# Two-layer cross-attention and feed-forward kernel: a scale folded into its weights, forty early zero-matmuls, constants by reductions, another order

## The chip, the cores and the metric

The kernel runs on one core of one Trainium2 chip. The metric is device time in microseconds (us), the median of several runs. A core has five engines that work side by side, each through its own queue and in order: TensorE (PE, matrix products), VectorE (DVE), ScalarE (ACT), GpSimd (POOL) and SyncE (SP, which here issues the transfers). They wait for each other by semaphores.

## The reference

The input x has 128 sequences of 64 tokens with 128 features; the context has the same shape. Four blocks follow each other, each added to x:

```
x = x + xattn0(layernorm(x), ctx, ctx)   # 16 heads of 8; q, k, v from normalised inputs;
                                         # softmax(q k^T / sqrt(8)) v; @ Wo + bo;
                                         # times sigmoid(qn @ Wg), then a layer norm
x = x + ffn0(layernorm(x))               # h = silu(w1 x * s1) * (w2 x * s2)
                                         # h = gelu(h1 h * s); h = gelu(h2 h * s)
                                         # out = (w3 h) * w3_s
x = x + xattn1(layernorm(x), ctx, ctx)   # 16 heads, plain softmax attention, @ w_o^T + b_o
x = x + ffn1(layernorm(x))               # relu(x W1 + b1) W2 + b2
```

The ffn weights h1 and h2 are 512 x 512, w3 is 128 x 512. `w3_s` is a vector of 128 factors, one for each output feature, so it may be applied to the output or to the columns of the weights.

## The kernel before, in words

The 8192 tokens are cut into 17 chunks: one of 256 tokens, fifteen of 512, one of 256. Each chunk goes through four stages, written as Python generators: `attention0`, `ffn0`, `attention1`, `ffn1`. A chunk of 512 tokens has two halves in each attention. All weights stay in on-chip memory; x, context and work tiles rotate through numbered slots.

A half of an attention goes like this. Scores come from PE (L658). DVE takes the negated maximum over keys (L662). DVE or POOL splits it into three bf16 parts (L672 to L675). PE transposes these (L679), ACT copies the result (L682). PE computes the scores again, transposed, with the maximum subtracted (L691). ACT exponentiates (L696). PE multiplies with the values (L710). ACT and DVE sort out the two heads that share a tile (L720 to L724), DVE takes the reciprocal of the sums (L727, L728), POOL multiplies (L742), and PE applies the output weights (L770). A layer norm is moments on DVE (L541, L543), an inverse root on POOL (L526 to L559) and the scaling on ACT (L568) or DVE (L572). PE transposes the result (L582).

In `ffn0` the two first products are L903 and L904, tanh is on ACT (L907), the gating on DVE (L909, L910). The square products are done with seven block products instead of eight (L956), for which POOL forms differences of inputs (L938) and sums of weights (L896). At its end the product with w3 (L770) stands in a PSUM bank. DVE multiplies it by `w3_s` into a work tile (L1046), and POOL adds that tile to x (L1048). In `ffn1` the products are L1080 and L770.

The order of all instructions is planned when the program is built. The class `Order` keeps a clock for each engine and for each slot, and gives each operation a length from a table (`LENGTHS`). Of all operations whose inputs are planned, it issues next the one that can start first; ties go by priority. To that priority a random draw is added, seeded by one number for each stretch of 50 us of planned time (`DRAWS`; a seed of 0 adds nothing). What comes out is one fixed queue for each engine.

At the start PE has nothing to do, so it multiplies a tile of zeros (L428): 60 matmuls before anything else, and more wherever the plan shows PE idle in its first 95 us (`RAMP`). Constants are made on DVE meanwhile: `masks` sums a table of 0 and 1 over two of its axes (L479 to L483), `folds` adds column groups of the identity (L799 to L804) and widens the result to `asel` (L808). POOL blanks three value tiles with memsets (L496, L498).

Of the kernel before, what the change touches and what calls it, by code (L numbers as in the profile page):

```python
# [26 lines left out]
HS = 4  # L27
# [11 lines left out]
for _n, _w in _COLS:  # L39
# [10 lines left out]
N_VB, N_NM = 3, 4  # L50
# [11 lines left out]


STRETCH = 50.0
DRAWS = [97, 0, 427, 0, 249, 0, 0, 0, 575, 0, 0, 112, 0, 817, 0, 39, 412, 0, 615, 329, 0, 15, 762, 0]
SPREAD = 0.1
SWAP = [*range(16, 32), *range(16)]

# [2 lines left out]
PE, DVE, ACT, POOL, SP = "PE", "DVE", "ACT", "POOL", "SP"  # L71
NONE = ""
# [8 lines left out]
        "product": (0.865, -0.2), "f1": (0.865, -0.2),  # L81
    },
    DVE: {
        "bias+": 0.28, "masks": 1.2, "gate weights": 0.4, "folds": 1.9, "moments": 1.07, "z": 1.3, "copied": 0.68,
        "scaled": 0.75, "qx": 1.5, "kx": 1.5, "vb": 1.8, "max": 2.3, "parts": 0.8, "reciprocal": 2.2, "o2": 0.83,
        "from bank": 0.68, "gate sums": 1.3, "gate": 0.4, "gained": 1.1, "gated": 1.45, "sum": 0.68, "saved": 0.68,
        "relu": 0.7,
# [235 lines left out]
def kernel(  # L323
# [16 lines left out]
    nc = tc.nc  # L340
# [7 lines left out]
    const = ctx.enter_context(tc.tile_pool(name="const", bufs=1))  # L348
# [8 lines left out]
    def tile_of(slot, shape, dtype=F32):  # L357

        kind, i = slot
        n = 1  # L360
        for d in shape[1:]:
            n *= d
        if kind == "bank":
            t = banks[:, i, :]
            t = t[:, 0:n] if dtype is F32 else t.bitcast(dtype)[:, 0:n]
        else:
            t = work.tile([P, COLUMNS[kind]], dtype, tag=f"{kind}{i}", name=f"{kind}{i}")[:, 0:n]
        if len(shape) == 2:
# [37 lines left out]
    order = Order(RESOURCES)  # L406
# [3 lines left out]
    hm = load("hm", [P, 2, 2, 2], headmask.rearrange("p (n s t) -> p n s t", n=2, s=2))  # L410
# [7 lines left out]
    w3 = load("w3", [P, 4, D], w_3)  # L418
# [7 lines left out]
    def busy(n, bank):  # L426
        for _ in range(n):
            nc.tensor.matmul(banks[:, bank, 0:P], blank, blank, start=True, stop=True)  # L428

    order.busy = busy  # L430
    busy(60, 7)
    ident = const.tile([P, P], F32, tag="ident", name="ident")
    make_identity(nc, ident)

    mask = const.tile([P, 4], F32, tag="mask", name="mask")
    half_mask = const.tile([P, 2, 4], F32, tag="half_mask", name="half_mask")
    im, pm = (lambda i: mask[:, i : i + 1]), (lambda i: mask[:, 2 + i : 3 + i])
    neg_half = const.tile([P, NG], F32, tag="neg_half", name="neg_half")
    nc.gpsimd.memset(neg_half, -0.5)
# [19 lines left out]
    def rowv(name, ng):  # L459
        return each(row[:, ROW[name], :], ng)  # L460
# [15 lines left out]

    def masks():
        yield Op(DVE, "masks")
        nc.vector.tensor_tensor(half_mask[:, 0, 0:2], hm[:, 0, 0, :], hm[:, 0, 1, :], ALU.add)  # L479
        nc.vector.tensor_tensor(half_mask[:, 1, 0:2], hm[:, 1, 0, :], hm[:, 1, 1, :], ALU.add)  # L480
        nc.vector.tensor_tensor(half_mask[:, 0, 2:4], hm[:, 0, :, 0], hm[:, 0, :, 1], ALU.add)
        nc.vector.tensor_tensor(half_mask[:, 1, 2:4], hm[:, 1, :, 0], hm[:, 1, :, 1], ALU.add)
        nc.vector.tensor_tensor(mask, half_mask[:, 0, :], half_mask[:, 1, :], ALU.add)  # L483
        for t, i, name in (
            (bk0, 2, "L0_xattn_bk"), (bq0, 0, "L0_xattn_bq"), (bk1, 2, "L1_xattn_b_k"), (bq1, 0, "L1_xattn_b_q"),
        ):
            nc.vector.tensor_scalar(t, mask[:, i : i + 2], colv(name), None, ALU.mult)

    def blanks():

        for i in range(N_NM):
            yield Op(POOL, "blank", put=[("nm", i)])
            nc.gpsimd.memset(nmax[i], 0.0)
            if i < N_VB:
                yield Op(POOL, "blank values", put=[("vb", i)])
                nc.gpsimd.memset(vblk[i], 0.0)  # L496
                for par in range(2):
                    nc.gpsimd.memset(vblk[i][64 * par : 64 * par + 64, :, 1, par, :], 1.0)  # L498
# [1 line left out]
    ones = const.tile([P, P], F32, tag="ones", name="ones")  # L500
    gw = const.tile([P, D + 1], F32, tag="gw", name="gw")
    identb = const.tile([P, P], BF16, tag="identb", name="identb")
    fold = const.tile([P, 2, 32], F32, tag="fold", name="fold")
    asel = const.tile([P, HS, P], BF16, tag="asel", name="asel")
    half_s1 = const.tile([P, 4], F32, tag="half_s1", name="half_s1")
    half_s12 = const.tile([P, 4], F32, tag="half_s12", name="half_s12")
# [249 lines left out]
    def token_major(blocks, ng, free, own=False):  # L756

        pe = None
        for g in range(ng):
            op = yield Op(  # L760
                PE,
                "tokens" if len(blocks) == 1 else "tokens 4",
                get=None if pe else {"bank": 1, "wk": 1} if own else {"bank": 1},
                put=free if g == ng - 1 else (),
            )
            if pe is None:
                pe = op
                ps = tile_of(pe.slots["bank"][0], (P, ng, D))
            for n, (lhs, w) in enumerate(blocks):
                nc.tensor.matmul(  # L770
                    ps[:, g, :],
                    lhs(g),
                    w,
                    start=(n == 0),
                    stop=(n == len(blocks) - 1),
                )
        return (ps, pe.slots["bank"], pe.slots["wk"]) if own else (ps, pe.slots["bank"])
# [16 lines left out]
    def folds():  # L794

        yield Op(DVE, "folds")

        nc.vector.tensor_copy(identb, ident)
        nc.vector.tensor_tensor(  # L799
            fold, ident[:, 0:64].rearrange("p (r c) -> p r c", r=2), ident[:, 64:128].rearrange("p (r c) -> p r c", r=2), ALU.add  # L800
        )
        nc.vector.tensor_tensor(fold[:, 0, :], fold[:, 0, :], fold[:, 1, :], ALU.add)
        for j in range(1, 3):
            nc.vector.tensor_tensor(  # L804
                fold[:, 0, 0:8], fold[:, 0, 0:8], fold[:, 0, 8 * j : 8 * j + 8], ALU.add
            )
        for s in range(HS):
            nc.vector.tensor_copy(  # L808
                asel[:, s, :].rearrange("p (j k) -> p j k", j=2),
                fold[:, 0, 2 * s : 2 * s + 2].unsqueeze(2).to_broadcast([P, 2, 64]),  # L810
            )

        nc.vector.tensor_scalar(half_s1, col[:, COL["L0_ffn_w1_s"]], 0.5, None, ALU.mult)
        nc.vector.tensor_tensor(half_s12, half_s1, col[:, COL["L0_ffn_w2_s"]], ALU.mult)
# [68 lines left out]
    def weights(l):  # L883

        a = [[wh[:, l, 2 * j : 2 * j + 2, 256 * i : 256 * i + 256] for j in range(2)] for i in range(2)]
        s = [ws[:, l, n] for n in range(3)]
        for out, x, y, f in (
            (s[0], a[1][0], a[1][1], ALU.add),  # L890
            (s[1], s[0], a[0][0], ALU.subtract),
            (a[1][0], a[0][0], a[1][0], ALU.subtract),
            (s[2], a[0][1], s[1], ALU.subtract),
        ):
            yield Op(POOL, "weights")
            nc.gpsimd.tensor_tensor(out, x, y, f)  # L896

        made_weights[l] = [a[0][0], a[0][1], s[2], a[1][1], s[0], s[1], a[1][0]]

# [115 lines left out]
    def ffn0(ci, prio):  # L1015
        xt, ng = x_sb[ci], GROUPS[ci]
        z, fz = yield from normalised(xt, ng)
        zT, fz = yield from transposed(z, ng, fz)
        fz = Last(fz, 4)
        b, made = {}, []  # L1020
        n = ng * P
        yield from two_halves(b, n)
        for k in range(4):
            made.append((yield (gated(k, zT, n, fz, b), prio)))
        yield made[:1]
        h = [Both(made[0], made[1]), Both(made[2], made[3])]
# [8 lines left out]
        ps, fp, fw = yield from token_major(  # L1035
            [
                (lambda g, k=k: b[k // 2][0][:, 2 * g // ng, k % 2, g * P % (n // 2) : g * P % (n // 2) + P], w3[:, k, :])
                for k in range(4)
            ],
            ng,  # L1040
            b[0][1] + b[1][1],
            own=True,
        )
        yield Op(DVE, "from bank", put=fp)
        y = tile_of(fw[0], (P, ng, D))
        nc.vector.tensor_tensor(y, ps, rowv("L0_ffn_w3_s", ng), ALU.mult)  # L1046
        yield Op(POOL, "add", put=fw)
        nc.gpsimd.tensor_tensor(xt, xt, y, ALU.add)  # L1048


    def context1(ci, got, prio):
# [68 lines left out]
    landed = [Op(SP, "load") for _ in range(9)]  # L1120
# [76 lines left out]
```

## Time and profile before

| what | value |
|---|---|
| median of three runs | 1130.64 us (1130.12 to 1131.97) |
| the profiled execution | 1132.17 us |
| its span, first to last instruction | 1130.3 us |
| PE busy | 1100.1 us (97%), 13871 matmuls |
| weight loads on PE | 868.5 us |
| DVE busy | 866.8 us |
| ACT busy | 726.0 us |
| POOL busy | 504.9 us |
| mean granted clock of PE | 0.996 |
| transfers | 23.23 MB, mean 21 GB/s |

All durations below are of the profiled execution. "Busy" of PE counts from a matmul's start to its modelled end. The time of the whole is the span and 1.9 us around it. The "chain" of the profile is found by going back from the last instruction, at each step to what released it or to the instruction before it on its engine.

### The profile page before, as it was taken

How to read it: one execution, taken by the hardware profiler on the slowest of the kernel's cores; microseconds unless marked ns; L12 is line 12 of the kernel's file. 1: busy time of each engine (PE TensorE's matmuls, PEld its weight loads, DVE VectorE, ACT ScalarE, POOL GpSimd, SP SyncE). 2: the span in 40 equal slices, each digit the busy share in tenths (PEclk: the TensorE clock that was granted, in tenths of full speed). 3: DMA queues.
4: the chain of work that ended last, by engine and by line, in shares of the span. 5: the costliest groups of instructions: out<-in, count | busy, mean ns of one | idle time of the engine just before them, and what ended most of it. 6: DMA issues, size and time to landing. Idle time of an engine off the chain costs nothing.

```text
span 1130.3 us, 32935 instructions
## 1 busy us (share of the span) xinstructions
PE 1100.1 (97%) x13871; PEld 868.5 (77%) x13871; DVE 866.8 (77%) x2139; ACT 726.0 (64%) x1279; POOL 504.9 (45%) x882
## 2 busy tenths in 40 slices
PE   7699999999999999999999999999999999999998
PEld 6577687778876778878676887777778887789786
DVE  7887969889877777567978687788789888643773
ACT  5467767666775776576646686667867675545553
POOL 6745545445534445333326355335345546352221
PEclk9999999999999999999999999999999999999999
DMA  7001000000001001001100000000000000000001
GB/s 244 12 2 29 21 11 21 11 1 20 12 2 34 2 2 39 1 3 38 49 20 20 11 21 11 12 19 12 11 11 12 11 7 11 1 1 1 12 20 43
DMA packets 35444, 23.23 MB, mean 21 GB/s; under 512 B 1504, under 2 KB 34272, under 8 KB 35168
## 3 DMA queue, kind: packets, MB, share of 16 engines
q1 hardware_dynamic: 35296, 21.13, 6.3%
q8 instruction: 109, 1.79, 0.7%
q14 instruction: 39, 0.32, 0.1%
HBM read 16.93 MB, written 4.19 MB: 19 GB/s over the span
## 4 chain that ended last, share of the span: by engine, by line
PE 87%; DVE 9%; ACT 2%; issue 1%; POOL 1%; DVEq 0%; ACTq 0%; POOLq 0%
PE banks L956 33%; PE banks L770 12%; PE banks L691 7%; PE banks L710 5%; PE banks L658 5%; PE banks L1080 5%; PE banks L903 4%; PE banks L904 4%; PE banks L582 4%; DVE m L662 3%; PE banks L631 3%; PE banks L618 2%; PE banks L606 2%; DVE su L727 1%; PE banks L428 1%
## 5 line engine op out<-in xcount | busy, mean ns | idle before, releaser
L662 DVE TENSOR_REDUCE m<-banks 128x32 f32<-128x2048 f32 x64 | 145.9, 2281 | 17.6 <-PE banks L658 16.9
L742 POOL TENSOR_TENSOR wk<-av,rec 128x256 f32<-128x256 f32 x64 | 46.9, 733 | 220.6 <-DVE rec L728 198.0
L696 ACT ACTIVATE e<-banks 128x2048 f32<-128x2048 f32 x64 | 120.2, 1877 | 36.3 <-PE banks L691 29.1
L956 PE MATMUL banks<-hd,wh 128*128 128x256 f32 (+1 forms) x544 | 127.7, 371 | 0.4 <-DVE wk L909 0.4
L956 PE MATMUL banks<-wk,wh 128*128 128x256 f32 (+1 forms) x544 | 127.5, 371 | 0.0
L956 PE MATMUL banks<-wk,ws 128*128 128x256 f32 (+1 forms) x544 | 126.3, 371 | 0.8 <-POOL wk L938 0.7
L727 DVE RECIPROCAL su<-su 128x256 f32<-128x256 f32 x64 | 111.5, 1742 | 0.0
L956 PEld LDWEIGHTS banks<-wk,wh 128*128 128x128 f32 x544 | 96.4, 190 | 18.0 <-issue 5.7
L975 ACT ACTIVATE hd<-hd,col 128x256 f32<-128x256 f32 (+1 forms) x204 | 88.8, 488 | 31.7 <-DVE hd L982 30.9
L956 PEld LDWEIGHTS banks<-hd,wh 128*128 128x128 f32 x544 | 95.4, 190 | 16.4 <-issue 4.1
L956 PEld LDWEIGHTS banks<-wk,ws 128*128 128x128 f32 x544 | 94.7, 190 | 16.5 <-issue 3.3
L982 DVE TENSOR_TENSOR hd<-banks,hd 128x512 f32<-128x512 f32 (+1 forms) x102 | 66.7, 656 | 52.9 <-PE banks L956 45.3
L529 POOL TENSOR_TENSOR nr<-nv,neg_half 128x4 f32<-128x4 f32 (+1 forms) x102 | 99.7, 978 | 8.5
L938 POOL TENSOR_TENSOR wk<-hd,wk 128x512 f32<-128x512 f32 (+1 forms) x68 | 82.4, 1212 | 40.4 <-DVE hd L910 29.0
L512 ACT COPY hd<-banks 128x512 f32<-128x512 f32 (+1 forms) x68 | 37.9, 557 | 73.0 <-PE banks L956 67.9
L568 ACT ACTIVATE wk<-x,nb,nr 128x128 f32<-128x128 f32 x192 | 79.0, 484 | 7.1 <-POOL nb L559 6.8
L658 PEld LDWEIGHTS banks<-kx,qx 32*128 32x128 f32 x2048 | 62.8, 186 | 22.4 <-issue 10.0
L710 PEld LDWEIGHTS banks<-e,vblk 128*32 128x32 f32 x4096 | 60.2, 110 | 24.0 <-issue 7.6
L658 PE MATMUL banks<-kx,qx 32*128 32x128 f32 x2048 | 74.6, 282 | 2.5 <-ACT qx L597 1.2
L710 PE MATMUL banks<-e,vblk 128*32 128x64 f32 x4096 | 70.4, 220 | 2.2 <-ACT e L696 2.2
L691 PE MATMUL banks<-qx,kx 32*128 32x128 f32 x2048 | 71.7, 277 | 0.0
L909 DVE SCALAR_TENSOR_TENSOR wk<-wk,banks 128x512 f32<-128x512 f32 (+1 forms) x68 | 43.9, 646 | 33.1 <-ACT wk L907 33.0
(136 smaller groups left out, 2399.2 us busy)
## 6 DMA issues: line engine op xcount, KB each, us to landing
c<-in_c_dram SPq DMA_DIRECT2D x30, 256.0 KB, 3.0
x<-in_x_dram SPq DMA_DIRECT2D x15, 256.0 KB, 3.6
out_dram<-x SPq DMA_DIRECT2D x15, 256.0 KB, 2.3
wh<-in_w_h_dram SPq DMA_DIRECT2D x1, 2048.0 KB, 12.4
c<-in_c_dram SPq DMA_DIRECT2D x4, 128.0 KB, 2.7
wa<-in_w_a_dram SPq DMA_DIRECT2D x2, 256.0 KB, 5.1
w<-in_w_dram SPq DMA_DIRECT2D x1, 512.0 KB, 7.9
wf<-in_w_f_dram SPq DMA_DIRECT2D x2, 256.0 KB, 6.7
```

The lines of the kernel that those rows point to most:

```text
L529: nc.gpsimd.tensor_tensor(rs, ve, neg_half[:, 0:ng], ALU.pow)
L568: nc.scalar.activation(z[:, g, :], src[:, g, :], AF.Identity, bias=nb[:, g : g + 1], scale=rs[:, g : g + 1])
L658: nc.tensor.matmul(sc[:, g, s, :], qs[h, s, :], ks[h, s, :], start=True, stop=True)
L662: nc.vector.tensor_reduce(m, sc.rearrange("p g s (j k) -> p g (s j) k", j=2), AX.X, ALU.max, negate=True,)
L691: nc.tensor.matmul(sT[:, g, s, :], lhs, rhs, start=(n == 0 and s == 0), stop=(n == 1), skip_group_check=True)
L696: nc.scalar.activation(e.rearrange("p g s i q -> p (g s i q)"), sT.rearrange("p g s c -> p (g s c)"), AF.Exp, scale=SCALE,)
L710: nc.tensor.matmul(po[32 * g : 32 * g + 32, i, s, :], vb[:, 4 * (half * HS + s) + g, i : i + 2].rearrange("p h j d -> p (h j d)"), e[:, g, ...
L727: nc.vector.reciprocal(su, su)
L770: nc.tensor.matmul(ps[:, g, :], lhs(g), w, start=(n == 0), stop=(n == len(blocks) - 1),)
L938: nc.gpsimd.tensor_tensor(T[m][0], x(), y(), ALU.subtract)
L956: nc.tensor.matmul(pieces[bank][0][:, o], w[:, k, o * P : (o + 1) * P], x[:, k], start=(new and k == 0 and o == 0), stop=(k == 1), skip_gr ...
L975: nc.scalar.activation(out(i, t)[:, o], (src or out(i, t))[:, o], AF.Gelu, scale=colv(scale, 2 * i + o))
```

## The change

Five things change.

- `w3_s` is multiplied once into the w3 weights, on POOL, after the weight sums of the second square layer. At the end of `ffn0` one DVE addition of the PSUM bank and x takes the place of the DVE product and the POOL addition.
- PE starts with 40 zero-matmuls instead of 60, and the planner's clock of PE starts at 2.5 us instead of 0.
- `masks` and `folds` use reductions over two axes and one widening copy instead of chains of small additions; their planned lengths are lowered.
- The memset of the last value tile may be planned only from 24 us on (`landed[7]`).
- All 24 seeds of the draws are new, and none is zero, so that the planned order differs on every engine from the start to the end.

```diff
-DRAWS = [97, 0, 427, 0, 249, 0, 0, 0, 575, 0, 0, 112, 0, 817, 0, 39, 412, 0, 615, 329, 0, 15, 762, 0]
+DRAWS = [36508, 23866, 23866, 23866, 23866, 23866, 23866, 23866, 23866, 23866, 23866, 23866, 23866, 23866, 23866, 61831, 23866, 23866, 61347, 23866, 22251, 23866, 8812, 23866]
...
-    busy(60, 7)
+    busy(40, 7)
+    order.clock[PE] = 2.5
...
-        nc.vector.tensor_tensor(half_mask[:, 0, 0:2], hm[:, 0, 0, :], hm[:, 0, 1, :], ALU.add)
...
-        nc.vector.tensor_tensor(mask, half_mask[:, 0, :], half_mask[:, 1, :], ALU.add)
+        for i, order_of in ((0, "p n s t -> p t n s"), (2, "p n s t -> p s n t")):
+            nc.vector.tensor_reduce(mask[:, i : i + 2], hm.rearrange(order_of), AX.XY, ALU.add)
...
             if i < N_VB:
+                if i == N_VB - 1:
+                    yield Op(NONE, "free", after=landed[7])
                 yield Op(POOL, "blank values", put=[("vb", i)])
...
-        nc.vector.tensor_tensor(fold[:, 0, :], fold[:, 0, :], fold[:, 1, :], ALU.add)
...
+        rows_of_8 = ident.rearrange("p (r j c) -> p c r j", j=4, c=8)[:, :, :, 0:3]
+        nc.vector.tensor_reduce(fold, rows_of_8, AX.XY, ALU.add)
+        nc.vector.tensor_copy(
+            asel.rearrange("p s (j k) -> p (s j) k", j=2), fold.unsqueeze(2).to_broadcast([P, 2 * HS, SEQ])
         )
...
+        if l == 1:
+            yield Op(POOL, "weights")
+            nc.gpsimd.tensor_tensor(w3, w3, rowv("L0_ffn_w3_s", 4), ALU.mult)
...
-            own=True,
         )
         yield Op(DVE, "from bank", put=fp)
-        y = tile_of(fw[0], (P, ng, D))
-        nc.vector.tensor_tensor(y, ps, rowv("L0_ffn_w3_s", ng), ALU.mult)
-        yield Op(POOL, "add", put=fw)
-        nc.gpsimd.tensor_tensor(xt, xt, y, ALU.add)
+        nc.vector.tensor_tensor(xt, ps, xt, ALU.add)
```

More of the change, by code (lines that the diff above doesn't have):

```diff
@@ L83 @@
     DVE: {
-        "bias+": 0.28, "masks": 1.2, "gate weights": 0.4, "folds": 1.9, "moments": 1.07, "z": 1.3, "copied": 0.68,
+        "bias+": 0.28, "masks": 0.9, "gate weights": 0.4, "folds": 1.3, "moments": 1.07, "z": 1.3, "copied": 0.68,
         "scaled": 0.75, "qx": 1.5, "kx": 1.5, "vb": 1.8, "max": 2.3, "parts": 0.8, "reciprocal": 2.2, "o2": 0.83,
@@ L435 @@
     mask = const.tile([P, 4], F32, tag="mask", name="mask")
-    half_mask = const.tile([P, 2, 4], F32, tag="half_mask", name="half_mask")
     im, pm = (lambda i: mask[:, i : i + 1]), (lambda i: mask[:, 2 + i : 3 + i])
@@ L478, in masks @@
         yield Op(DVE, "masks")
-        nc.vector.tensor_tensor(half_mask[:, 0, 0:2], hm[:, 0, 0, :], hm[:, 0, 1, :], ALU.add)
-        nc.vector.tensor_tensor(half_mask[:, 1, 0:2], hm[:, 1, 0, :], hm[:, 1, 1, :], ALU.add)
-        nc.vector.tensor_tensor(half_mask[:, 0, 2:4], hm[:, 0, :, 0], hm[:, 0, :, 1], ALU.add)
-        nc.vector.tensor_tensor(half_mask[:, 1, 2:4], hm[:, 1, :, 0], hm[:, 1, :, 1], ALU.add)
-        nc.vector.tensor_tensor(mask, half_mask[:, 0, :], half_mask[:, 1, :], ALU.add)
+        for i, order_of in ((0, "p n s t -> p t n s"), (2, "p n s t -> p s n t")):
+            nc.vector.tensor_reduce(mask[:, i : i + 2], hm.rearrange(order_of), AX.XY, ALU.add)
         for t, i, name in (
@@ L502 @@
     identb = const.tile([P, P], BF16, tag="identb", name="identb")
-    fold = const.tile([P, 2, 32], F32, tag="fold", name="fold")
+    fold = const.tile([P, 2 * HS], F32, tag="fold", name="fold")
     asel = const.tile([P, HS, P], BF16, tag="asel", name="asel")
@@ L798, in folds @@
         nc.vector.tensor_copy(identb, ident)
-        nc.vector.tensor_tensor(
-            fold, ident[:, 0:64].rearrange("p (r c) -> p r c", r=2), ident[:, 64:128].rearrange("p (r c) -> p r c", r=2), ALU.add
-        )
-        nc.vector.tensor_tensor(fold[:, 0, :], fold[:, 0, :], fold[:, 1, :], ALU.add)
[L803 to L811, printed above, removed]
+        rows_of_8 = ident.rearrange("p (r j c) -> p c r j", j=4, c=8)[:, :, :, 0:3]
+        nc.vector.tensor_reduce(fold, rows_of_8, AX.XY, ALU.add)
+        nc.vector.tensor_copy(
+            asel.rearrange("p s (j k) -> p (s j) k", j=2), fold.unsqueeze(2).to_broadcast([P, 2 * HS, SEQ])
+        )
         nc.vector.tensor_scalar(half_s1, col[:, COL["L0_ffn_w1_s"]], 0.5, None, ALU.mult)
@@ L1034, in ffn0 @@
         yield ready[0] + ready[1]
-        ps, fp, fw = yield from token_major(
+        ps, fp = yield from token_major(
             [
```

## The prediction

> **What bounds the kernel now.** I read the busy shares first, then the stages, then who waited for whom on TensorE (PE), then the chain of waits through the first 100 us.
>
> ```profile
> PE 1100.1 (97%) x13871; PEld 868.5 (77%) x13871; DVE 866.8 (77%) x2139; ACT 726.0 (64%) x1279; POOL 504.9 (45%) x882
> ```
>
> PE is idle for 1130.3 - 1100.1 = 30.2 us. Nothing that the other engines save counts unless it shortens those 30 us, or takes useless instructions off PE. The stages say where they lie (after each length: busy us of PE, PEld, DVE, ACT, POOL, then the granted clock):
>
> ```profile
> 0.00:10.00 10.00, 8.74 (x104) 8.55 (x104) 6.20 (x43) 2.67 (x5) 6.68 (x22) 1.00 0.65 178
> 20.00:30.00 10.00, 7.19 (x233) 6.13 (x232) 7.71 (x21) 5.77 (x12) 3.45 (x7) 1.00 0.47 125
> 40.00:60.00 20.00, 14.95 (x152) 11.25 (x152) 16.73 (x43) 8.33 (x16) 14.82 (x30) 0.85 0.05 14
> 500.00:600.00 100.00, 96.49 (x1404) 72.83 (x1403) 81.30 (x207) 61.05 (x100) 30.66 (x54) 1.00 0.11 31
> 900.00:1000.00 100.00, 100.00 (x1191) 79.61 (x1191) 74.88 (x172) 62.05 (x102) 46.59 (x78) 1.00 0.02 6
> 1000.00:1050.00 50.00, 50.00 (x368) 44.48 (x367) 20.43 (x44) 24.95 (x59) 19.13 (x29) 1.00 0.01 1
> 1120.00:1130.30 10.30, 6.65 (x53) 5.93 (x51) 1.12 (x2) 1.64 (x4) 0.00 (x0) 0.95 0.13 40
> ```
>
> Length minus PE busy, added over all stages: 15.8 us before 100 us, 10.8 us from 100 to 1000 us, none from 1000 to 1120 us, 3.6 us at the end (last add and store, which stay). So there are two places to gain: the ramp, and some ten stalls in the middle. In the ramp PE also executes most of its 217 zero-matmuls, 17.8 us busy. The middle's stalls are these (waits of PE after 100 us: total, times, longest):
>
> ```profile
> PE banks L679 <- DVE nmax L675: 4.0, 4, 1.4
> PE banks L770 <- DVE m L662: 2.7, 1, 2.7
> PE banks L679 <- POOL nmax L675: 1.3, 2, 1.0
> ```
>
> They are the softmax maximum: scores (L658), maximum on DVE (L662), its split into parts (L672 to L675), then its transpose (L679), behind which PE's whole queue stands. The chain of the start (start, length, what):
>
> ```profile
> 0.98 6.40 PE banks L428 x67
> 7.38 0.28 PE banks L790 x2
> 7.66 1.56 PE banks L428 x28
> 9.22 0.24 PE banks L582 x2
> ...
> 50.62 1.35 ACT qx L597 x2
> 51.97 0.04 issue
> 52.01 1.22 PE banks L658 x32
> 53.25 2.30 DVE m L662
> ```
>
> Until 9 us PE is late only because of its own zeros. The first normalised tile stood ready at 6.45 us (ACT L568, 5.57 plus 0.88), and its transpose came at 9.06. Later the ramp is a chain of latencies over DVE, POOL and ACT, with PE waiting.
>
> **The change, part by part.**
>
> *Scale folded into w3.* Removed per chunk: DVE L1046 (684 ns) and POOL L1048 (1275 ns). Added per chunk: one DVE add of the nearest row's kind (L1075, 685 ns). DVE: 0. POOL: 15 x 1.275 + 2 x 0.726 = 20.6 us less, plus one 1.27 us product (row L896). POOL is 45% busy, so no time directly.
>
> ```profile
> L1048 POOL TENSOR_TENSOR x<-x,wk 128x512 f32<-128x512 f32 x15 | 19.1, 1275 | 41.9 <-DVE wk L1046 38.9 <-DVE gate L842 3.1
> L1046 DVE TENSOR_TENSOR wk<-banks,row 128x512 f32<-128x512 f32 x15 | 10.3, 684 | 18.1 <-PE banks L770 18.0
> ```
>
> Each chunk's next moments start 1.3 us earlier. DVE had waited 10.0 us for that add, 7 times, but no PE wait names it: I take 0, between 0 and 2 us of gain (a share of the 10.8). The one w3 product stands in POOL's queue after the weight sums of the second square layer and right before the parts of chunk 2's first maximum. By the stepping below it is done at 55.5 us, the parts at 56.5, while PE has other work to 57.4: 0, at most 1.3 us if that cover is gone. w3 is first read after 80 us.
>
> *Constants.* Four fold instructions (0.22, 0.20, 0.37 for two) and four copies (0.63) become one reduction over 12 of 128 columns per output and one copy; five mask sums (five of 0.15 to 0.17) become two reductions. No such small reduction is in the trace. Bounds: 0.15 us (the smallest DVE rows) and 0.3 us (96 inputs at 2281/2048 = 1.1 ns each is 0.11, plus 0.15 fixed). I take 0.25 each, and 0.5 for the copy: about 0.9 us less on DVE before 7.7 us. It is then caught by a transfer: the moments of x of chunk 1 waited for their DMA until 9.35 us. So 0, with 0.5 us either way.
>
> *Zeros: 60 became 40.* By the 107 ns pitch (49 up to 6.18 us; 56 ns after), 40 end at 5.25, the gate product (0.3) at 5.55, the next 18 at 6.9. PE is free 2.1 us earlier at this point. In all, 204 stand where 217 did.
>
> *Order.* Both programs' listings give the same useful matmuls, 350 instead of 353 changes between PE's array modes, and much moved work. Counted by rows: 18 more normalisations on DVE (0.43 each), fewer key and query maskings there: DVE about +3 us. ACT: 10 fewer table loads (1.283 each), 18 fewer normalisations, 10 more maskings: about -20 us. SP issues the same 80 instructions. The last memset of a value tile (1.38 + 0.6 us, L496 and L498) moves behind the first maximum's parts on POOL.
>
> *Ramp, stepped along the new order with these rows' durations.* x of chunk 0 now goes first through POOL: moments end at 4.80, POOL's five small steps take 1.63 (3.90 to 5.53 before), ACT 0.88: transpose at 7.6 instead of 9.06. But DVE does the query mask after x of chunk 1 (10.5), then 0.98 and 0.54; values and keys 1.15; keys' mask on ACT 1.1: first scores at 14.2, before 14.13. The lead is gone there. It returns in chunk 1: its scores come at 20.9 and 24.5 (before 22.53 and 26.18), the third maximum ends at 27.9 (before 32.1). Chunk 2's normalised context again comes late (43.6, before 43.3), since two halves' products stand ahead of its moments on DVE; PE sits about 3.5 us idle. Then the difference: chunk 0's feed-forward tile is normalised on ACT at 47.6, ahead of chunk 2's query mask instead of behind it (51.84), and the first w1 product (L903) starts at 49.9 instead of 56.56. Before, 2.4 us of chunk 2's scores had been done by then, so the true lead is 4.3 us. Chunk 2's softmax follows between the feed-forward's pieces. When chunk 1's feed-forward tile is transposed (67.6; before 70.54) PE has also done 3.4 us more useful work; before got that far at 75.9: a lead of 8.3 us. From 76.7 us to 120 us PE had no stall before, so a lead at that point is kept to the end, if the new order has no new stalls.
>
> *The clock takes a part back.* I stepped at full rate. The trace has two stretches at half rate (columns as above):
>
> ```profile
> 44.00:45.00 1.00, 0.65 (x4) 0.48 (x3) 1.00 (x2) 0.47 (x1) 1.00 (x2) 0.50 0.30 85
> 58.00:59.00 1.00, 1.00 (x5) 0.82 (x4) 0.90 (x4) 0.27 (x1) 0.78 (x4) 0.50 0.00 0
> ```
>
> They follow gaps of 1.4 us (at 40.7), and of 1.2 and 1.6 us (at 50.8 and 54.1), and each loses 1.7 us (the missing clock shares added). The Trainium skill (TensorE: Matmul & The Clock Gate, "What's actually happening") says that PE falls to half rate after an idle window of about 3.4 us. By the rule only the new order's 3.5 us gap would count: lead 8.3 - 1.7 = 6.6. By the trace shorter gaps suffice, and the new ramp has as many: 8.3 - 3.4 = 4.9. The measurement decides: 5 us, between 2 and 8. The same section asks about 3.4 us of steady work for full rate, which speaks against cutting zeros; here it took 5.2 us (0.98 to 6.18), and zeros and gate product run unbroken to 6.9. If it came a window later, 0.5 us.
>
> *Middle.* For each softmax half I added PE's work that stands between the scores and the transpose of the maximum in both listings. The chain needs about 3.5 us (2.2 + 1.1 + semaphores) if DVE is free. After the ramp, covers under 4 us: 9 halves before, 14 now; the shortest 1.9 before (the one near the 2.7 us stall), 3.4 now. So the 2.7 us stall goes, and five more short covers come, at 5.3/9 = 0.6 us each: -2.7 + 3.0 = 0. Range -8 to +10 us.
>
> *Sum.* The profiled execution took 1132.17 us, span 1130.3 plus 1.9 around it. 1132.2 - 5 + 0 = 1127.2. The median of the three runs stands 1.5 us under the profiled one: 1125.7.
>
> **Rivals.**
> 1. *The lead is lost in the ramp.* More zeros stand behind the first transpose than before (146, before 122: 24 x 0.056 = 1.3 us), and longer half-rate stretches eat the rest. For it: at the first scores my steps show no lead. Against: the feed-forward starts 4 us earlier by a plain exchange on ACT. Time about 1130.
> 2. *Slower: the maximum's transpose becomes the bound of the middle.* 14 short covers, each at the largest wait seen (1.4 us, L679), are 19.6 us instead of 10.8: +8.8, minus 5, is +3.8: 1134.5. It decides from about 1 us per short cover on. For it: DVE's order is in-line, and its 18 more normalisations stand ahead of maxima. Against: ACT and POOL are both freer by 20 us.
> 3. *The middle runs clean as well*: only 3 of 10.8 us of stalls stay: 1132.2 - 5 - 7.8 - 1.5 = 1118.
>
> **How the numbers follow.** Likeliest 0.50 (1123 to 1128); rival 3, 0.21; rival 1, 0.16; rival 2, 0.13. About 0.2% (2.3 us) can be told from no change here. Faster: 0.50 + 0.21 = 0.71; same 0.16; slower 0.13. The range runs from rival 3 with one us more of lead (1116) to a little short of rival 2 (1134).
>
> **What would show it.** Right: the first L582 near 7.6 us and first L903 near 50; all but one of the zero-matmuls before 65 us; PE idle before 100 us about 11 to 13 us; idle from 100 to 1000 us near 11 us; POOL about 486 us busy, ACT near 706. Wrong: a first L903 after 55 us, or L679 waiting more than 12 us in the middle.

## The result, and the profile after

The changed kernel takes 1136.88 us (median; 1136.32 to 1137.02) where the kernel before, run beside it, takes 1131.31 us (1130.12 to 1133.12). The ratio is 1.0043, interval 1.0031 to 1.0054: slower by 0.3 to 0.5%, where 1125.7 us had been predicted. The profiled execution took 1136.92 us with a span of 1134.9 us, 4.6 us more than before's span.

The busy shares of the changed kernel, the first line of its page:

```profile
PE 1104.3 (97%) x13858; PEld 870.4 (77%) x13858; DVE 866.4 (76%) x2139; ACT 704.5 (62%) x1252; POOL 487.2 (43%) x874
```

PE is idle for 1134.9 - 1104.3 = 30.6 us, before for 30.2 us. So nearly all of the 4.6 us is *busy* time of PE (4.2 us), with 13 matmuls fewer. PE did no more work; it did some of it more slowly. The stages show where (after each length: busy us of PE, PEld, DVE, ACT, POOL, then the granted clock):

```profile
0.00:10.00 10.00, 8.22 (x79) 7.43 (x79) 6.36 (x40) 3.49 (x6) 7.13 (x24) 1.00 0.68 191
20.00:30.00 10.00, 7.56 (x250) 6.70 (x250) 8.52 (x17) 4.67 (x8) 3.74 (x9) 1.00 0.42 115
40.00:60.00 20.00, 14.23 (x92) 9.63 (x89) 16.81 (x44) 8.37 (x17) 14.42 (x24) 0.83 0.05 14
60.00:80.00 20.00, 18.70 (x331) 16.29 (x332) 16.29 (x43) 10.21 (x18) 7.12 (x17) 0.83 0.01 2
80.00:100.00 20.00, 18.07 (x107) 13.53 (x106) 18.27 (x54) 14.78 (x36) 14.94 (x23) 1.00 0.10 27
500.00:600.00 100.00, 99.85 (x1227) 78.70 (x1226) 71.60 (x201) 68.86 (x123) 33.87 (x70) 1.00 0.12 33
900.00:1000.00 100.00, 99.47 (x1244) 77.67 (x1237) 76.70 (x168) 66.42 (x118) 43.70 (x82) 1.00 0.02 6
1000.00:1050.00 50.00, 50.00 (x362) 45.14 (x362) 21.95 (x48) 25.54 (x62) 20.72 (x29) 1.00 0.00 1
```

A granted clock of 0.83 over 20 us is a loss of 0.17 x 20 = 3.4 us, and it stands in two stages: two stretches at half rate (granted clock 0.50) of 6.8 us each (43.2 to 50.0, 60.3 to 67.1). Before had two of half that length, which lost 1.7 us each. The length less PE's busy time gives the idle time: 17.3 us before 100 us (before 15.8; 11 to 13 had been predicted), 9.3 us from 100 to 1000 us (before 10.8), none from 1000 to 1120 us, 4.0 us at the end. The middle is what was predicted, and its stalls are short and spread (waits of PE after 100 us, the three largest):

```profile
PE banks L678 <- DVE nmax L674: 1.6, 1, 1.6
PE banks L690 <- ACT e L695: 1.6, 2, 1.0
PE banks L690 <- DVE av L723: 1.1, 1, 1.1
```

To see where the lead went I added up PE's useful work (each matmul at a fixed length by its shape, zeros left out) and looked up when each amount had been reached, in us from the span's start:

| useful work done | 36 us | 45 us | 60 us | 100 us | 1031 us (nearly all) |
|---|---|---|---|---|---|
| before | 76.2 | 85.5 | 100.5 | 143.8 | 1126.3 |
| changed | 77.4 | 86.4 | 103.7 | 147.6 | 1130.5 |

At 100 us of work the changed kernel is 3.8 us behind, and from there on both need the same time (982.5 and 982.9 us). The whole loss lies in the first 148 us. Half rate is a part of it; the waits of PE between 40 and 100 us point to the rest:

```profile
PE banks L581 <- ACT wk L567: 2.6, 1, 2.6
PE banks L630 <- ACT wk L588: 1.9, 1, 1.9
PE banks L897 <- DVE wk L903: 1.6, 1, 1.6
PE banks L657 <- DVE m L661: 1.5, 1, 1.5
```

The first was foreseen (3.5 us had been predicted). The other three were not. Two of them follow one DVE group. DVE's timeline (start, length, engine, line, what), with the row of the kernel before as the last line:

```profile
52.82 4.63 DVE L563 SCALAR_TENSOR_TENSOR wk<-wk,mv,row 128x128 f32<-128x128 f32 x4
57.38 0.41 DVE L903 SCALAR_TENSOR_TENSOR wk<-wk,banks 128x256 f32<-128x256 f32 x1
57.89 0.48 DVE L904 SCALAR_TENSOR_TENSOR hd<-wk,half_s,banks 128x256 f32<-128x256 f32 x1
58.28 2.28 DVE L661 TENSOR_REDUCE m<-banks 128x32 f32<-128x2048 f32 x1
...
58.73 1.13 DVE L564 SCALAR_TENSOR_TENSOR wk<-wk,mv,row 128x128 f32<-128x128 f32 x4
```

The same four instructions take 4.63 us in place of 1.13. They scale a chunk's attention output and are wanted only at 65.9 us, but the gating (L903, L904) and the maximum (L661) stand behind them in DVE's queue. PE waits first for the gating and then for the maximum. POOL's timeline in these microseconds is one unbroken row of instructions that read and write the on-chip memory (SBUF), the new w3 product (L890) last:

```profile
52.22 1.27 POOL L839 TENSOR_TENSOR x<-x,row 128x512 f32<-128x512 f32 x1
53.44 1.32 POOL L887 TENSOR_TENSOR wh<-wh 128x512 f32<-128x512 f32 x1
54.72 1.31 POOL L887 TENSOR_TENSOR ws<-wh,ws 128x512 f32<-128x512 f32 x1
56.00 1.31 POOL L890 TENSOR_TENSOR w<-w,row 128x512 f32<-128x512 f32 x1
```

DVE's group ends at 57.45, just as POOL's row ends at 57.31. The chain that ended last runs through it (start, length, what):

```profile
52.91 4.54 DVE wk L563 x4
57.45 0.34 DVE wk L903
...
58.37 2.21 DVE m L661
60.58 0.04 issue
60.62 2.14 PE banks L657 x32
```

The third wait, 1.9 us at 96.5, has the same form. Four gate sums on DVE (L827, 0.28 us each at 71.6 us) meet three 128x512 differences of POOL:

```profile
92.54 0.42 DVE L976 TENSOR_TENSOR hd<-banks,hd 128x256 f32<-128x256 f32 x1 [0.40 <-PE banks L950]
92.88 1.00 DVE L827 SCALAR_TENSOR_TENSOR wk<-wk,gw 128x128 f32<-128x128 f32 x1
...
93.81 1.35 DVE L827 SCALAR_TENSOR_TENSOR wk<-wk,gw 128x128 f32<-128x128 f32 x1
...
95.30 1.34 DVE L827 SCALAR_TENSOR_TENSOR wk<-wk,gw 128x128 f32<-128x128 f32 x1
...
96.58 0.41 DVE L976 TENSOR_TENSOR hd<-banks,hd 128x256 f32<-128x256 f32 x1
```

```profile
92.46 1.28 POOL L932 TENSOR_TENSOR wk<-hd,hd 128x512 f32<-128x512 f32 x1
93.69 1.32 POOL L932 TENSOR_TENSOR wk<-hd 128x512 f32<-128x512 f32 x1
95.09 1.41 POOL L932 TENSOR_TENSOR wk<-hd,wk 128x512 f32<-128x512 f32 x1
```

The slow DVE instructions end within 0.15 us of POOL's ends (93.88, 95.16 and 96.64 against 93.74, 95.01 and 96.50). The fourth, not shown, started together with the last of POOL's three and took its usual 0.28 us. Behind them waits a short sum (L976), behind that on ACT a gelu (L969), behind that in ACT's queue the copy (L588) that PE's values need:

```profile
97.03 0.69 ACT L969 ACTIVATE hd<-hd,col 128x128 f32<-128x128 f32 x2 [1.68 <-DVE hd L976]
97.63 0.76 ACT L588 ACTIVATE wk<-banks,col 128x512 f32<-128x512 f32 x1
```

Before had no wait of PE above 0.4 us between 73 and 110 us.

The Trainium skill states what the rows suggest (SBUF — State Buffer, "Who interferes with whom"): a DVE instruction with two SBUF inputs contends with a GpSimd instruction that reads SBUF, and whichever comes second stands still until the other is through. L563 has its tile and the gain row in SBUF, L827 its tile and the gate weights. L976 has one input in PSUM, and its 0.42 us at 92.54 beside POOL's L932 is its usual length.

### The profile page after: what moved, and what is told of

The parts are those of the page before. It is cut to its first block, busy times and chain, and to the rows that moved or that the text cites. A ratio compares the mean times of both kernels' runs of the same rounds, so it can differ in the third digit from the quotient of the medians.

```text
span 1134.9 us, 32840 instructions
## 1 busy us (share of the span) xinstructions
PE 1104.3 (97%) x13858; PEld 870.4 (77%) x13858; DVE 866.4 (76%) x2139; ACT 704.5 (62%) x1252; POOL 487.2 (43%) x874
## 4 chain that ended last, share of the span: by engine, by line
PE 86%; DVE 9%; ACT 3%; issue 1%; POOL 0%; DMA 0%; SPq 0%; DVEq 0%; ACTq 0%
PE banks L950 33%; PE banks L769 12%; PE banks L690 6%; PE banks L657 6%; PE banks L709 5%; PE banks L1070 5%; PE banks L897 4%; PE banks L898 4%; PE banks L581 3%; PE banks L617 3%; PE banks L630 2%; PE banks L605 2%; DVE m L661 2%; DVE su L726 1%; ACT e L695 1%
## 5 line engine op out<-in xcount | busy, mean ns | idle before, releaser
L661 DVE TENSOR_REDUCE m<-banks 128x32 f32<-128x2048 f32 x64 | 146.0, 2281 | 20.6 <-PE banks L657 20.2
L969 ACT ACTIVATE hd<-hd,col 128x256 f32<-128x256 f32 (+1 forms) x204 | 88.4, 488 | 45.5 <-DVE hd L976 45.0
L976 DVE TENSOR_TENSOR hd<-banks,hd 128x512 f32<-128x512 f32 (+1 forms) x102 | 66.3, 655 | 48.0 <-PE banks L950 39.1
L932 POOL TENSOR_TENSOR wk<-hd,wk 128x512 f32<-128x512 f32 (+1 forms) x68 | 82.5, 1214 | 12.4 <-PE banks L605 3.8
L567 ACT ACTIVATE wk<-x,nb,nr 128x128 f32<-128x128 f32 x176 | 72.6, 487 | 4.6 <-POOL nb L558 4.2
L897 PE MATMUL banks<-wk,w 128*128 128x512 f32 (+1 forms) x136 | 68.6, 586 | 2.7 <-DVE wk L903 1.6
```

Of the source, the lines that this page charges most:

```text
L661: nc.vector.tensor_reduce(m, sc.rearrange("p g s (j k) -> p g (s j) k", j=2), AX.X, ALU.max, negate=True,)
L897: nc.tensor.matmul(pa, w12[:, 0, k * P : (k + 1) * P], zT, start=True, stop=True)
L932: nc.gpsimd.tensor_tensor(T[m][0], x(), y(), ALU.subtract)
L969: nc.scalar.activation(out(i, t)[:, o], (src or out(i, t))[:, o], AF.Gelu, scale=colv(scale, 2 * i + o))
```

## The experiments

All times are medians, with the ratio to the kernel before run beside each and its interval. The text before each measurement is what was expected of it. The changed kernel's own interval is 1.0031 to 1.0054. Those of experiments 1 to 3 overlap it, so their gains of 1.0 to 2.4 us are not clear of noise, and their traces say more than their times. Those of experiments 5 to 7 and 9 to 11 lie below it.

**1. POOL's sums of the second layer moved to the start.** The four sums are issued behind the last value tile's memset, and no longer at 46 to 56 us.

```diff
+                if i == N_VB - 1:
...
+                    nc.gpsimd.tensor_tensor(s[0], a[1][0], a[1][1], ALU.add)
+                    nc.gpsimd.tensor_tensor(s[1], s[0], a[0][0], ALU.subtract)
+                    nc.gpsimd.tensor_tensor(a[1][0], a[0][0], a[1][0], ALU.subtract)
+                    nc.gpsimd.tensor_tensor(s[2], a[0][1], s[1], ALU.subtract)
...
-            nc.gpsimd.tensor_tensor(out, x, y, f)
+            if l == 0:
+                nc.gpsimd.tensor_tensor(out, x, y, f)
```

> The changed kernel with its planned order, but the four weight sums of the second square layer are issued on POOL right after the last value tile's memset (about 21.7 us, where POOL waited 6 us for DVE) instead of between 46 and 56 us. Theory A (four DVE normalisations of chunk 1, L563, took 4.63 us instead of 1.13 because POOL ran without a break at 51 to 57.3 us on the same tiles' memory): they take 2 to 3 us, the third w1 product no longer waits 1.6 us, and the total falls by 1.5 to 5 us against the changed kernel (1132 to 1135.5). Rival B (the half clock rate from 43 to 50 us and 60 to 67 us alone is the loss): under 1 us of gain. Rival C (the middle is the loss): no gain before 100 us, the total moves either way.

1134.47 us, ratio 1.0027 (1.0016 to 1.0037). The scaled rows took 1.44 us, and the 1.58 us gap was gone. But the sums, now at 21.8 to 26.9 us, met other DVE instructions, the splitting of a maximum into its parts (the last two rows are the changed kernel's):

```profile
24.52 1.21 DVE L679 TENSOR_TENSOR m<-m,nmax 128x32 f32<-128x32 f32 x1
25.77 1.18 DVE L680 CAST nmax<-m 128x32 bf16<-128x32 f32 x1
...
24.20 0.19 DVE L672 TENSOR_TENSOR m<-m,nmax 128x32 f32<-128x32 f32 x1
24.43 0.18 DVE L673 CAST nmax<-m 128x32 bf16<-128x32 f32 x1
```

The next maximum, in line behind them, started at 27.39 us in place of 25.25, and the ramp came 2 us later. So one collision was exchanged for another, and the gain of 2.4 us is what the move left over.

**2. Only the w3 product moved to the start.**

```diff
+                if i == N_VB - 1:
+                    nc.gpsimd.tensor_tensor(w3, w3, rowv("L0_ffn_w3_s", 4), ALU.mult)
```

> The changed kernel with its planned order, but the one product of w3 with its scale is issued on POOL at about 21.7 us instead of at 56.0. Theory A: it was the last of the POOL instructions that held up L563, so that ends 1.3 us sooner, PE's wait of 1.6 us at 56.3 us falls to about 0.3: total 1 to 1.5 us less than the changed kernel (about 1135.5). Rival B or C: the same as the changed kernel, 1136.9.

1135.88 us, ratio 1.0037 (1.0025 to 1.0050). The scaled rows still took 4.70 us: they met three of the sums and the bias addition. The w3 product alone is not the cause.

**3. Zeros in the first gap.** In the gap of 2.6 us at 40.3 us, ahead of the third chunk's transpose, 44 more zero-matmuls.

```diff
+        if n >= 30 and len(self.log) > 20:
+            n += 44
```

> The changed kernel with its planned order and 44 more zero-matmuls behind the 37 that stand before chunk 2's first transpose, so that PE is not idle from 40.3 to 42.9 us. Theory B (the 2.6 us gap puts PE at half rate until 50 us): no half rate before 50 us, the first w1 product (L897) starts 2 to 3 us sooner than 52.96, total 1 to 3 us less. Theory A says that the same POOL and DVE work at 51 to 57 us then still stands in the way, and most of it is lost again: total within 1 us of the changed kernel. If gaps have nothing to do with the rate, half rate stays.

1135.58 us, ratio 1.0034 (1.0021 to 1.0047). The first half-rate stretch was gone, but gaps of 1.65 and 1.50 us stayed, and a half-rate stretch followed them. The first w1 product came at 51.05 us in place of 52.96, so the stretch that shows 3.4 us had held it up by 1.9. Of the whole time 1.3 us were gained.

**4. The old constants in the new order.** `masks` and `folds` are written as in the kernel before; the planned lengths, and so the order, are those of the changed kernel.

> The changed kernel with its planned order, with the constants made by the old small additions and four copies. DVE starts chunk 1's moments about 0.9 us later, but its x still lands no sooner than before. Prediction: the same as the changed kernel within 0.5 us (1136.4 to 1137.4). Rival (the reductions are slow and in the way): faster by over 1 us.

1137.12 us, ratio 1.0048 (1.0034 to 1.0062). The constants are worth nothing, as predicted. The profile of this run had half rate only at 44.1 to 47.5 and at 95.3 to 98.7 us: which gap is followed by half rate, and for how long, differs between executions. The gap at 93 us (here 1.94 us) was in it too.

**5. The scaled rows behind the second maximum.** Four DVE instructions change their place in DVE's queue; nothing else moves on any engine.

```diff
+            if abs(op.end - 50.99) < 0.3:
+                held_z.append(scaled_rows)
...
+        if held_z:
+            maxima.append(0)
+            if len(maxima) == 2:
+                held_z.pop()()
```

> The changed kernel, with four DVE instructions moved: the scaled rows of the third chunk (the scalar_tensor_tensor of 128x128 that took 4.63 us at 52.8 in the changed kernel, beside four back to back sums of POOL) are issued behind the second maximum, two maxima later, as the kernel before does it. All else is the same. Theory (a DVE instruction that meets POOL's sums on the memory sets the ramp back): the four take about 1.1 to 1.6 us there, the gap of 1.58 us ahead of the third first-layer product and the 1.50 us gap ahead of the scores behind it close, the feed-forward transpose of chunk 1 comes 2 to 4 us before the 77.4 us of the changed kernel, and the time is 1 to 3.5 us below the changed kernel's (1133.5 to 1136). Rival (the ramp's place is not kept, only stalls after 77 us count): the ramp is earlier but the time stays within 1 us of 1136.9. Second rival (the order as such is longer, wherever the stalls are): same.

1133.23 us, ratio 1.0010 (1.0002 to 1.0018): 3.7 us less than the changed kernel. Its DVE timeline:

```profile
58.77 2.28 DVE L670 TENSOR_REDUCE m<-banks 128x32 f32<-128x2048 f32 x1
60.97 1.15 DVE L565 SCALAR_TENSOR_TENSOR wk<-wk,mv,row 128x128 f32<-128x128 f32 x4
```

The four take 1.15 us, the gaps of 1.58 and 1.50 us shrink to under 0.5 us each, and the second half-rate stretch is gone. 36 us of useful work are done at 71.9 us in place of 77.4. (In this execution the first half-rate stretch was 3.4 us long, and one of 3.4 us followed the gap that ends at 92.9 us.)

**6. The gate sums behind the sum that waited for them.**

```diff
+        if abs(op.end - 85.01) < 0.3:
+            held_sums.append(gate_rows)
...
             nc.vector.tensor_tensor(out(i, t), pieces[bank][0], out(i, t), ALU.add)
+            if held_sums:
+                held_sums.pop()()
```

> The changed kernel, with four other DVE instructions moved: the gate sums (scalar_tensor_tensor of 128x128, 1.00, 1.35, 0.28 and 1.35 us at 92.9 in the changed kernel, beside three back to back differences of POOL) are issued behind the next sum from a bank (L976, 0.41 us), which in the changed kernel waited behind them until 96.58 and kept ACT's queue and with it PE's values (a gap of 1.93 us at 96.5). Theory (this stall is a part of the loss): the gap is below 0.7 us, no stretch of half rate follows it, and the time is 1 to 3.5 us below the changed kernel's 1136.9. Rival (the stall is covered later, as stalls of PE in the ramp seem to be): the gap closes and the time is within 1 us of 1136.9.

1134.77 us, ratio 1.0022 (1.0015 to 1.0029): 2.1 us less than the changed kernel. DVE's timeline:

```profile
92.44 0.42 DVE L982 TENSOR_TENSOR hd<-banks,hd 128x256 f32<-128x256 f32 x1 [0.47 <-PE banks L956]
92.78 1.36 DVE L829 SCALAR_TENSOR_TENSOR wk<-wk,gw 128x128 f32<-128x128 f32 x1
```

The sum goes at 92.44 in place of 96.58, and no gap over 0.5 us is left on PE there. The gate sums are as slow as they were (1.36, 0.28, 1.35 and 1.34 us); nobody waits for them now. So it is not the slow instruction that costs, but what stands behind it.

**7. Both moves.**

> Both moves in one kernel: the scaled rows behind the second maximum, and the gate sums behind the sum from a bank. Theory (the two collisions of DVE with POOL, and the half rate behind their gaps, are what the changed kernel lost): 3 to 7 us below the changed kernel, 1130 to 1134, so level with the kernel before (1131) or faster. Rival (only one of them counts): the time of that one alone. Rival (the order as such is longer): within 1.5 us of 1136.9.

1130.23 us, ratio 0.9987 (0.9981 to 0.9994): 6.7 us less than the changed kernel, a little more than the two apart (3.7 and 2.1), and faster than the kernel before. The two places account for the whole loss and more. In the profiles the span is 6.4 us shorter: PE is idle for 27.0 us in place of 30.6 and busy for 1101.5 in place of 1104.3, the second half-rate stretch being gone with the gaps before it.

A rival is that half rate alone made the loss. The mean granted clock of each execution, known to three decimals, lets one compare at the same clock. At 0.997 the new order takes 1135.9 us (two executions of experiment 4), with the scaled rows moved 1133.1 (three), with both moved 1130.6 (13), and the kernel before 1131.5 (52). So most of the loss is there at an equal clock too.

**8. The fold in the old order.** The kernel before, with `w3_s` in the weights.

```diff
+        if l == 1:
+            nc.gpsimd.tensor_tensor(w3, w3, rowv("L0_ffn_w3_s", 4), ALU.mult)
...
-        nc.vector.tensor_tensor(y, ps, rowv("L0_ffn_w3_s", ng), ALU.mult)
+        nc.vector.tensor_tensor(xt, ps, xt, ALU.add)
...
-        nc.gpsimd.tensor_tensor(xt, xt, y, ALU.add)
```

> The kernel before, in its own order, with the last scale of the first feed-forward multiplied into its weights as the change does (one product of 128x512 more on POOL behind the sums of layer 1, ten multiplications of DVE turned into additions, POOL's ten additions of 1.28 us gone). Theory (the fold itself is worth nothing, the loss is that of the new order): within 1.5 us of the kernel before. Rival (the fold costs, by its product among POOL's sums in the ramp or by the additions): slower by 2 us or more. Second rival (it helps where POOL's adds stood in the way): faster by 2 us or more.

1131.77 us, ratio 0.9997 (0.9989 to 1.0006). (The additions in question are 17, one for each chunk; the "ten" in the expectation is a slip.) The fold takes 19 us off POOL (486.0 us busy in place of 504.9), and no change of the time shows. With experiments 4 and 11 this leaves the order as the place of the loss.

**9. POOL's three instructions left out.** The third and fourth sum and the w3 product are missing, and the second sum stands in where the fourth is used. This separates the collision from the place in the queue: the scaled rows stay where the changed kernel has them.

```diff
+            if l == 0 or out is s[0] or out is s[1]:
                 nc.gpsimd.tensor_tensor(out, x, y, f)
...
-            nc.gpsimd.tensor_tensor(w3, w3, rowv("L0_ffn_w3_s", 4), ALU.mult)
...
-        made_weights[l] = [a[0][0], a[0][1], s[2], a[1][1], s[0], s[1], a[1][0]]
+        made_weights[l] = [a[0][0], a[0][1], s[1 if l == 1 else 2], a[1][1], s[0], s[1], a[1][0]]
```

> The changed kernel in its own order on every engine; left out are three of POOL's instructions: the third and fourth sum of the second layer's weights and the product of w3 with its scale (1.32, 1.31 and 1.31 us at 53.4 to 57.3), so its output is another. No DVE instruction is moved. Theory (the scaled rows on DVE are slow because they meet these on the memory): the four instructions of L563 take 1.1 to 2.6 us (the bias add of POOL before them still stands) in place of 4.63, the gaps of 1.58 and 1.50 us close or halve, and the time is 1.5 to 4 us below the changed kernel's, near the 1133.2 of the kernel that moved them. Rival (what counted was their place in DVE's queue): L563 stays above 3.5 us, and the time is within 1 us of 1136.9.

1132.69 us, ratio 1.0004 (0.9996 to 1.0013), 4.2 us less than the changed kernel. Its DVE row:

```profile
52.96 1.80 DVE L563 SCALAR_TENSOR_TENSOR wk<-wk,mv,row 128x128 f32<-128x128 f32 x4
```

1.80 us in place of 4.63 (the bias addition of POOL still stands beside it), in the same place of the queue. The length came from POOL's neighbours.

**10. Both moves, and the zeros at 40 us.**

> Both DVE moves, and 44 more zero-matmuls in PE's queue in the gap of 2.6 us at 40.5, ahead of the third chunk's transpose. Theory (the stretch at half rate at 44 to 50 that follows the gap costs what it shows, 3 us): no half rate between 40 and 60, 1 to 3.5 us below the 1130.2 of both moved, so 1127 to 1129.2. Rival (half rate there is covered, since PE has gaps behind it until 53): within 0.7 us of 1130.2.

1128.40 us, ratio 0.9970 (0.9958 to 0.9981), the fastest of all. The windows of the kernel with both moves, and of this one (columns as above):

```profile
40.00:50.00 10.00, 7.20 (x32) 4.96 (x30) 7.37 (x33) 4.40 (x10) 6.98 (x18) 0.67 0.09 26
50.00:60.00 10.00, 8.98 (x103) 6.97 (x103) 7.93 (x14) 4.31 (x9) 8.94 (x12) 0.99 0.01 2
```

```profile
40.00:50.00 10.00, 9.01 (x89) 6.84 (x86) 8.97 (x36) 5.51 (x12) 7.81 (x18) 1.00 0.09 28
50.00:60.00 10.00, 8.55 (x104) 6.89 (x102) 8.33 (x13) 3.88 (x8) 8.21 (x13) 1.00 0.00 1
```

The half-rate stretch showed 3.4 us of lost clock share; taking it away gave 1.8 us. The first w1 product came 2.1 us sooner (51.04 in place of 53.17). PE's timeline shows where the rest went: at full rate PE waits for POOL and DVE.

```profile
45.13 1.16 PE L784 MATMUL banks<-wa,wk 128*128 128x128 f32 x8 [0.38 <-POOL wk L756]
48.95 1.12 PE L616 MATMUL banks<-wk,wa 128*128 128x512 f32 x2 [0.31 <-DVE wk L601]
```

At half rate the first of these waits is 0.14 us and the second is none. The four transposes at 43.1 us take nearly as long at full rate (1.48 us, at half rate 1.63), since at full rate PE stands for 0.06 us before each of the last three until ACT has its tile.

**11. Both moves, with sixty zeros at the start.**

```diff
-    busy(40, 7)
+    busy(60, 7)
```

> Both DVE moves, with sixty zero-matmuls at the start as in the kernel before, in place of forty. Theory (PE's first transpose waits in line behind them, and the lead so lost is kept): PE is free 2.1 us later, the first scores come 0.5 to 2 us later, and the time is 0.5 to 2 us above the 1130.2 of both moved. Rival (loads and DVE hold the first scores whichever number stands there): within 0.5 us of 1130.2. Second rival (sixty keep the clock up where forty leave a gap): below 1129.7.

1130.12 us, ratio 0.9987 (0.9980 to 0.9993), the same as with forty. PE's first scores came at 14.38 us in place of 13.53, and the 0.85 us do not show in the median. (Before's profile had them at 14.13, the changed kernel's at 13.32.)

**12. The control: the kernel before with zeros in its own gaps.**

```diff
+        n += {(28, "transpose"): 24, (14, "scores"): 20, (12, "transpose"): 26}.get((n, op.name), 0) if t > 30 else 0
```

The third entry adds nothing, since no bank is free for zeros in that gap.

> The kernel before in its own order, with 24 more zero-matmuls in its gap of 1.44 us at 40.4 and 20 more in that of 1.24 us at 50.3; its gap of 1.61 us at 53.6 stays as it is. Theory (half rate behind a gap costs what it shows): the stretch at half rate at 44 to 47 (1.7 us lost) is gone, that at 57.7 to 60.9 may stay, and the time is 1 to 2 us below the kernel before. Rival (half rate is covered in this order by PE's later gaps at 50.3 and 53.6, where the maxima set the time): within 0.7 us of the kernel before.

1130.85 us, ratio 0.9988 (0.9980 to 0.9996). No half rate is left between 40 and 64 us (the profiled execution has a stretch of 3.4 us at 542 us, where before's had none). A part of the last gain is therefore to be had in either order. With no half rate in either ramp the new order, collisions moved, is still ahead: ratio 0.9970 (0.9958 to 0.9981) against 0.9988 (0.9980 to 0.9996), each against the kernel before. The intervals just touch, but all six times of the one (up to 1129.32 us) lie under all fourteen of the other (from 1129.46).

The useful work of these kernels, as in the table above (us from the start):

| useful work done | 36 us | 60 us | 100 us | 500 us | 1031 us |
|---|---|---|---|---|---|
| before | 76.2 | 100.5 | 143.8 | 571.1 | 1126.3 |
| before, zeros in gaps | 73.8 | 98.1 | 141.4 | 570.3 | 1125.4 |
| changed | 77.4 | 103.7 | 147.6 | 571.4 | 1130.5 |
| scaled rows moved | 71.9 | 99.8 | 143.7 | 567.5 | 1126.7 |
| both moved | 72.7 | 97.1 | 141.0 | 564.9 | 1124.0 |
| both moved, zeros at 40 us | 70.5 | 95.0 | 138.9 | 562.7 | 1121.8 |

With the rows moved the lead that was predicted does appear in the ramp (4.3 us at 36 us of work), and the second collision, with the half rate behind its gap, eats most of it before 60 us. In the old order the lead from the zeros, 2.4 us, shrinks to 0.8 us by 500 us of work. In the new order with both moves the lead from the zeros is 2.2 us at 36 us of work and still 2.2 us at the end.

## Why the prediction was wrong, step by step

- *Fold, constants, zeros at the start: 0 each.* Right within the noise, by experiments 8, 4 and 11. POOL's 487.2 and ACT's 704.5 us are near the predicted 486 and 706; DVE did not grow by the 3 us that its listing gave (866.4). The lengths of the constants were only near: 0.31 us for the large reduction, 0.15 for each small one (0.25 was taken).
- *First steps of the ramp.* Right: first transpose at 7.25 us (7.6 predicted), first scores at 13.32 (14.2), the next two at 20.42 and 24.00 (20.9 and 24.5), the gap ahead of chunk 2's transpose 2.6 us (3.5).
- *First L897 at 49.9 us.* It came at 52.96, neither under 50 nor over 55. Of the 3.1 us 1.9 are the half-rate stretch of 43.2 to 50.0 (experiment 3), which the prediction had put into a sum apart. The other 1.2 us belong to the stepping, in a step that no run separates.
- *Chunk 1's feed-forward transpose at 67.6 us, a lead of 8.3 us.* This step failed. The transpose came at 77.44: 3.1 us from the step above, and 6.8 us more, against which the trace shows the gaps of 1.58, 1.50 and 0.6 us and a second half-rate stretch that lost 3.4. The term that was mis-sized is the four scaled rows on DVE, stepped with before's duration (1.13 us; measured 4.63). That row had been taken where POOL's sums were not beside it. The prediction noted that the w3 product joins POOL's queue there, and asked only whether POOL would be late with the maximum's parts; it did not ask what POOL's run of five instructions does to DVE beside it. Experiments 5 and 9 take the cause away on either side and give 3.7 and 4.2 us. With both moves and the zeros (experiment 10) the transpose comes at 70.53, so 2.9 us of this step's miss stay open. Before's own trace has the slow form too: four of these rows at 762.01 us took 3.49 us beside POOL, and over all 64 the mean is 492 ns with a median of 347.
- *The clock takes 3.4 us.* The right mechanism, mis-sized: the profiled run lost 6.8 us, while taking one stretch away gives only 1.3 to 1.8 us of the 3.4 it shows. The lead of 8.3 us set a ramp stepped at full rate against a measured one that had itself lost 3.4. With no half rate on either side, and the collisions moved, the new order is 73.8 - 70.5 = 3.3 us ahead at 36 us of work.
- *"A lead at that point is kept to the end, if the new order has no new stalls."* The condition did not hold: the stall of 1.93 us at 96.5 is new. Experiment 6 gives 2.1 us for it.
- *The middle, 0 (range -8 to +10).* Right: 9.3 us idle where 10.8 stood; 982.9 us for the useful work from 100 to 1031 us against 982.5. Rival 2 put the loss into the maximum's transpose (L678); that waits 1.6 us in all in the middle. The time was slower, as in rival 2, by another mechanism.
- *Rival 1, the lead lost in the ramp*, was nearest in kind, but it stopped at no gain (1130 us). It named longer half-rate stretches, which came, and more zeros behind the first transpose, which no run takes out (experiment 11 tests the zeros ahead of it).

Left open: the 2.9 us above. How much of experiment 5's gain comes from the gaps and how much from the half rate behind them is known only roughly: at an equal clock the two kernels are 2.8 us apart, in their medians 3.7.

## What to carry to other kernels

When a new order is stepped with an old order's durations, ask of each row what ran beside it. A DVE instruction with two inputs in SBUF has no length of its own while POOL works through a row of SBUF instructions (1.13 us became 4.63 here), and in before's trace a mean far above the median (492 ns against 347) was the sign of it. Then look at what stands behind it in its queue: a slow instruction that nobody waits for cost nothing, and two such groups, moved behind what they held up, turned 0.43% slower into 0.13% faster. A lead in a ramp has to be followed until the stage where PE no longer waits for anything; here that was 148 us, and 2.6 of the 3.8 us of lag arose after the point at which the prediction stopped stepping (36 us of useful work).

## What the runs showed of the hardware

- DVE's scalar_tensor_tensor of 128x128 with two SBUF inputs takes 0.28 us alone and 1.34 to 1.36 us when it comes beside POOL's 128x512 tensor_tensor: it ends with POOL's instruction. POOL's own lengths grew little (1.27 to between 1.28 and 1.41 us). Sums with a PSUM input kept their lengths beside POOL (0.42 us). Two small instructions of 128x32 on SBUF, one of them a cast with a single input, took 1.21 and 1.18 us beside POOL in place of 0.19 and 0.18 (experiment 1).
- A maximum read from PSUM took 2.29 us at 54.68 (experiment 5) beside the same row of POOL instructions, as long as alone.
- PE fell to half rate after some of its gaps of 1.4 to 2.7 us. Every stretch whose clock shares were added up between 40 and 102 us lost 1.7 or 3.4 us, so it was about 3.4 or 6.8 us long, one or two of the windows of about 3.4 us of which the Trainium skill speaks (TensorE: Matmul & The Clock Gate, "What's actually happening"). That the windows run freely, as it says, fits too: after the same gap of 1.9 us at 91 to 98 us half rate followed in four profiled executions (experiments 2, 4, 5 and 9), and in three it did not (the changed kernel, experiments 1 and 3); after the 2.7 us gap at 538 us it followed in experiment 12 and not in the kernel before. But no gap here was as long as such a window, and an idle stretch of one window, as its table asks, was not needed.
